# FFN weights gathered in reorder-index order, tokens permuted by one-hot matmuls; norms and scalings of the attention stage on ScalarE

## The chip, the cores and the metric

The kernel runs on one core of one Trainium2 chip, as one launch. A core has five engines with an instruction queue each: TensorE (PE: matmuls and transposes), VectorE (DVE), ScalarE (ACT: activation functions and copies), GpSimd (POOL: elementwise work, and the gathers by index, which it issues), and SyncE (SP), which here only issues DMAs. Each queue runs in the order in which the program was built; queues wait for each other through semaphores. The metric is the device time of one execution in microseconds (us). A run's figure is a median of several executions.

## The reference, cut to what matters

A decoder layer over 4 x 256 = 1024 tokens of width 256: a Mamba block with a mixture of experts, cross attention to 64 context tokens, and an FFN with emulated 8-bit weights and activations. Each is followed by a residual sum and a layernorm. The change touches the last two.

```python
x = layernorm(x + mamba_moe(x))                  # 512 inner channels, 8 experts, top 2
# cross attention, 16 heads of 128
q = rmsnorm((x @ Wq) per head) * gq              # eps 1e-5 inside the rsqrt
k = rmsnorm((ctx @ Wk) per head) * gk
attn = softmax(q @ k.T / sqrt(128))
x = layernorm(x + (attn @ (ctx @ Wv)) @ Wo)
# FFN
def reorder_quantize(x, idx):
    scale = max(abs(x)) / (448 * 6)
    xr = (x / scale)[:, idx]                     # columns gathered by idx
    scale_x = max(abs(xr), per row) / 448
    return fp8(xr / scale_x), scale_x, scale
def qlinear(qx, sx, s, W, idx, out_idx=None):
    Wr = W[:, idx]
    ws = max(abs(Wr), per row) / 448
    y = qx * sx @ (fp8(Wr / ws) * ws).T * s
    return y if out_idx is None else y[:, out_idx]
qx = reorder_quantize(x, up_idx)                 # up_idx: 256 entries
g = qlinear(*qx, w_gate, up_idx, out_idx=down_idx)    # 704 outputs
u = qlinear(*qx, w_up,   up_idx, out_idx=down_idx)
qt = reorder_quantize(silu(g) * u, down_idx)     # down_idx: 704 entries
x = layernorm(x + qlinear(*qt, w_down, down_idx))
```

## The kernel before, in words

Tokens lie in 8 tiles of 128 (`NT`), each token a partition, in `x_sb`. The program is one function, `decoder_kernel`, and runs in stages. A **manual order** (`tc.manual_schedule`) keeps the instructions of PE, DVE, ACT and POOL as they are written in the scan, MoE and combine stages; in the last stage (attention and FFN) the framework's scheduler orders each engine's queue when the program is built.

**Scan** (to about 315 us): the Mamba recurrence, DVE scans with POOL products and PE sums.

**Preparation of K** (`prep_k`, to about 400 us): weights of queries and keys are multiplied together into `m_d` in DRAM, so that scores are one matmul with the tokens. Its last copies `mst` leave by DMA at L785.

**MoE** (about 400 to 613 us): 23 slots (`NSLOT`) of 128 gathered rows. The loop over `s` at L1165 calls `slot_rows` (transposes of the gathered rows, L1109, and two copies, one on ACT, L1111, one on DVE, L1112), `slot_up` (the matmuls `p_gu` at L1121), `slot_act` and `slot_down` (L1144 to L1160). After each slot, `next(fill, None)` runs one piece of `prep_ffn`, which makes the FFN's weights beside the MoE. Its first piece runs ahead of slot 0 (L1163). `prep_ffn` begins with `counts`: an iota on POOL (L949), one-hot matrices of the two index lists on DVE (L962), their column sums on PE (`p_cnt`, L969), which give how often each column is named (`cnt_up`, `cnt_dn`) and a 0/1 mask of those that are named (`mask_up`, `mask_dn`); the transposes `p_cntc` (L977) turn the counts into columns. Then, six times for the up weights (`gather`, `round_gu`, `turn_gu`) and twice for the down weights (`round_dn`, `turn_dn`), the rows are gathered, masked, scaled, rounded, transposed, multiplied by the counts, and written to DRAM as two bf16 parts: a high part and the rest that the product with a count leaves (index j = 0, 1 of `wgu_d`, `wdn_d`). So no token is ever permuted: a column named twice has its weight doubled.

**Combine** (about 613 to 649 us): 16 gathers of expert outputs on POOL's queue (L1214), their sum and a layernorm on DVE, and beside them the matmuls of V and Wo (`prep_v`). SP loads the FFN weights (L1219 to L1222).

**Attention and FFN** (about 649 us to the end): a loop of 11 steps (L1397). Step i runs `stage_scores(i)`, `stage_attend(i - 1)`, `stage_up(i - 2)` and `stage_down(i - 3)`: four tiles are in flight. In one step:

- `stage_scores`: transpose `p_x1T`, ACT copy `x1T` (L1275), query matmuls `p_q` (L1280), squares on ACT (L1285) and sums on DVE (`ssq`, L1286), `rq` = 1/rms (L1290, through `rsqrt_mean`: DVE, DVE, ACT square root), score matmuls `p_sc` (L1295), then the softmax on `v` (128x1024): DVE product (L1302), DVE maximum (L1305), POOL subtraction (L1306), ACT exponential (L1307), DVE sum (L1308), POOL product (L1310).
- `stage_attend`: transposes `p_aT`, ACT copies, matmuls `p_av` (L1327), DVE residual sum (L1330), `layernorm` (L68): statistics, `rsqrt_mean`, and a DVE scaling (L76).
- `stage_up`: POOL mask `xm` (L1347), `quantize` (L1333: maximum, scaling at L1340, `round_fp8` at L78: two DVE operations and two POOL ones), transpose `p_xqT`, ACT copy `xqT` (L1353), matmuls `p_gu` (L1361, 16 of 352 columns), DVE scaling `gu`, SiLU on ACT (L1368), DVE product `tb`.
- `stage_down`: `quantize` of `tb`, transposes `p_tT`, ACT copies `tT`, matmuls `p_fo` (L1386, 12), residual sum, `layernorm`, store.

ACT changes its function table (`ACT_TABLE_LOAD`) whenever it goes between square root, exponential and SiLU; copies need no change.

Of the kernel before, what the change touches and what calls it, by code (L numbers as in the profile page):

```python
# [10 lines left out]
F32 = mybir.dt.float32  # L11
I32 = mybir.dt.int32
AF = mybir.ActivationFunctionType
ALU = mybir.AluOpType
# [3 lines left out]
P = 128  # L18
B, L, D = 4, 256, 256
T = B * L  # L20
NT = T // P
# [28 lines left out]
def decoder_kernel(  # L50
# [17 lines left out]
    def layernorm(buf, t, pool):  # L68

        st = pool.tile([P, 6], F32, tag="ln_st", name="ln_st", bufs=2)  # L70
        mv = pool.tile([P, 2], F32, tag="ln_mv", name="ln_mv", bufs=2)
        rs = pool.tile([P, 1], F32, tag="ln_rs", name="ln_rs", bufs=2)
        nc.vector.bn_stats(st, buf[:, t, :])
        nc.vector.bn_aggr(mv, st)
        rsqrt_mean(rs, mv[:, 1:2], 1, EPS_LN)
        nc.vector.tensor_scalar(buf[:, t, :], buf[:, t, :], mv[:, 0:1], rs, sub, mult)  # L76

    def round_fp8(o, q, m):  # L78
# [6 lines left out]
        nc.gpsimd.tensor_tensor(q, q, m, add)  # L85
        nc.gpsimd.tensor_tensor(o, q, m, sub)
# [47 lines left out]


    mask_up = const.tile([P, D], F32, name="mask_up")
    cnt_up = const.tile([P, KD], F32, name="cnt_up")
    cnt_dn = const.tile([P, NI], F32, name="cnt_dn")
# [566 lines left out]

    wgu_d = dram.tile([2, P, KD, 2, I], BF16, name="wgu_d")
    wdn_d = dram.tile([2, P, NI, D], BF16, name="wdn_d")
# [238 lines left out]
    def counts(ps, pool, mask_dn):  # L946
# [5 lines left out]
        for idx, n, cnt, mask in ((idx_up, D, cnt_up, mask_up), (idx_dn, I, cnt_dn, mask_dn)):  # L952
# [3 lines left out]
            row = pool.tile([P, I], F32, tag="wd_m", name="cntrow")  # L956
            parts = [(0, n)] if n <= HALF else [(0, n // 2), (n // 2, n - n // 2)]
            for o2, w2 in parts:
# [13 lines left out]
                nc.scalar.copy(row[:, o2 : o2 + w2], pt[:, 0:w2])  # L972
            nc.vector.tensor_scalar(mask, row[:, 0:n], 1.0, None, ALU.min)
            yield
            pc = ps.tile([P, HALF], F32, tag="ps", name="p_cntc")
            for i, (o, w) in enumerate(chunks):
                nc.tensor.transpose(pc[:w, i * 32 : i * 32 + 32], row[0:32, o : o + w], ident[0:32, 0:32])  # L977
            for i, (o, w) in enumerate(chunks):
                nc.scalar.copy(cnt[:w, i : i + 1], pc[:w, i * 32 : i * 32 + 1])

    def prep_ffn(fw, ps):

        mask_dn = fw.tile([P, I], F32, name="mask_dn")
        yield from counts(ps, fw, mask_dn)
        mcol = fw.tile([P, NI], F32, name="mcol")
        nc.vector.tensor_scalar(mcol[:, 0 : NI - 1], cnt_dn[:, 0 : NI - 1], 1.0, None, ALU.min)
        nc.vector.tensor_scalar(
            mcol[0 : ICH[-1][1], NI - 1 :], cnt_dn[0 : ICH[-1][1], NI - 1 :], 1.0, None, ALU.min  # L990
        )

        def gather(i):
# [4 lines left out]
                in_offset=bass.IndirectOffsetOnAxis(ap=idx_dn[:w, i : i + 1], axis=0),  # L998
# [3 lines left out]
        def round_gu(i, wt):  # L1002
# [9 lines left out]
            round_fp8(wb[:w], wt[:w], m[:w])  # L1012
            nc.vector.tensor_scalar_mul(sc[:w, 0, 1:2], sc[:w, 0, 1:2], mcol[:w, i : i + 1])
# [4 lines left out]
        def turn_gu(i, wb):  # L1018
# [6 lines left out]
            st = fw.tile([P, 2, KD, 2, P], BF16, tag="w_st", name="w_st", bufs=2)  # L1025
            for k in range(KD):

                src = pt[:, k * 2 * w : (k + 1) * 2 * w].rearrange("p (g o) -> p g o", o=w)
                c = cnt_up[:, k : k + 1]
                nc.vector.tensor_scalar_mul(st[:, 0, k, :, 0:w], src, c)  # L1030
                nc.vector.scalar_tensor_tensor(st[:, 1, k, :, 0:w], src, c, st[:, 0, k, :, 0:w], mult, sub)
            for j in range(2):
                for k in range(KD):
                    nc.sync.dma_start(wgu_d[j, :, k, :, o : o + w], st[:, j, k, :, 0:w])

        def round_dn(r, wt):
# [7 lines left out]
            round_fp8(wb, wt, m)  # L1044
# [3 lines left out]
        def turn_dn(r, wb):  # L1048
# [3 lines left out]
            st = fw.tile([P, 2, NI, P], BF16, tag="wd_st", name="wd_st", bufs=1)  # L1052
            nc.gpsimd.memset(st[I - (NI - 1) * P :, :, NI - 1, :], 0.0)
            for i, (o, w) in enumerate(ICH):
                c = cnt_dn[:w, i : i + 1]
                src = pt[:w, i * P : (i + 1) * P]
                nc.vector.tensor_scalar_mul(st[:w, 0, i, :], src, c)
                nc.vector.scalar_tensor_tensor(st[:w, 1, i, :], src, c, st[:w, 0, i, :], mult, sub)
            for j in range(2):
                nc.sync.dma_start(wdn_d[j, :, :, r * P : (r + 1) * P], st[:, j])  # L1060
# [139 lines left out]
    wgu = [lt2.tile([P, KD, 2, I], BF16, name=f"wgu{j}") for j in range(2)]  # L1200
    wdn = [lt2.tile([P, NI, D], BF16, name=f"wdn{j}") for j in range(2)]
# [5 lines left out]
    with ExitStack() as cctx, tc.manual_schedule(engines={ET.PE, ET.DVE, ET.Activation, ET.Pool}):  # L1207
# [10 lines left out]
        for j in range(2):  # L1218
            nc.sync.dma_start(wgu[j], wgu_d[j])  # L1219
            nc.sync.dma_start(wdn[j], wdn_d[j])  # L1220
        nc.sync.dma_start(sgu_row, sgu_d.unsqueeze(0).to_broadcast([P, 2, I]))
        nc.sync.dma_start(sdn_row, sdn_d.unsqueeze(0).to_broadcast([P, D]))  # L1222
# [35 lines left out]
    with ExitStack() as xctx:  # L1258
# [9 lines left out]
        def stage_scores(t):  # L1268
# [8 lines left out]
            for q in range(H // GQ):  # L1277
# [10 lines left out]
                )  # L1288
            rq = wk2.tile([P, H], F32, tag="rq", name="rq")
            rsqrt_mean(rq, ssq, HD, EPS_A)  # L1290
# [187 lines left out]
```

## Time and profile before

| what | us |
|---|---|
| median of 3 runs (lowest, highest) | 852.98 (850.94, 855.36) |
| the profiled execution, its own time | 856.38 |
| its span, first to last instruction | 854.7 |
| MoE's first expert matmul | 402.12 |
| first query matmul of the last stage | 650.09 |
| query matmuls of tiles 1 to 7 begin | 663.12, 679.59, 698.52, 724.15, 746.23, 768.40, 790.57 |
| busy PE, DVE, ACT, POOL over the span | 685.7, 569.1, 341.4, 385.9 |

The profile is one execution. A page gives busy times and the costliest groups; the chain of work follows the execution back from its last instruction, step by step to what released each; the timeline lists instructions with start and duration in us, and in brackets how long the engine was idle before and what released it. A name such as `xT<-p_xT` is output and inputs, a line number such as L1112 is a line of the kernel before. Ends of matmuls are modelled, and a float32 matmul is listed as two.

### The profile page before, as it was taken

Reading aid. Unit: us, or ns where it says so; the run is one execution under the profiler, and the core shown is the slowest. Engines: PE = TensorE matmul, PEld = TensorE weight load, DVE = VectorE, ACT = ScalarE, POOL = GpSimd, SP = SyncE. Lnnn points to the kernel's source line nnn. Section 1 sums busy time; section 2 is a strip of 40 time slices with the busy share of each in tenths; the row PEclk is TensorE's granted clock in tenths of the full one; section 3 lists DMA queues with packets and bytes.
Section 4 is the critical chain, followed back from the end, with each engine's and each line's share of the span. In section 5 each row is a group of like instructions: output and inputs, shape, how many; then the busy total and the mean of one; then the engine's idle time right before and its main releaser. Section 6 shows DMA issues by size and latency. Waiting matters only on the chain.

```text
span 854.7 us, 8109 instructions
## 1 busy us (share of the span) xinstructions
PE 685.7 (80%) x2449; PEld 383.5 (45%) x2449; DVE 569.1 (67%) x959; ACT 341.4 (40%) x564; POOL 385.9 (45%) x278
## 2 busy tenths in 40 slices
PE   3968868778656776747999999999986998999963
PEld 1533433324322323635555656556642554555541
DVE  4468799997899993663335454555144578888885
ACT  3386654755533323322221112112233555555533
POOL 7039878899766860022012332222060334444451
PEclk9999998999877997767999999999997999999985
DMA  4023322256521308943022544232690101000000
GB/s 153 1 74 86 99 65 69 83 156 205 168 87 44 104 25 298 397 142 104 25 72 17 67 55 66 39 54 56 204 393 16 49 1 49 7 6 7 8 6 19
DMA packets 54954, 76.43 MB, mean 89 GB/s; under 512 B 15872, under 2 KB 35072, under 8 KB 54144
## 3 DMA queue, kind: packets, MB, share of 16 engines
q1 hardware_dynamic: 48048, 64.11, 23.8%
q0 software_dynamic: 2320, 6.56, 5.2%
q10 hardware_dynamic: 4544, 5.24, 1.8%
q8 instruction: 21, 0.34, 0.2%
q14 instruction: 21, 0.17, 0.1%
HBM read 64.22 MB, written 11.67 MB: 89 GB/s over the span
## 4 chain that ended last, share of the span: by engine, by line
PE 45%; DVE 26%; POOL 12%; issue 7%; ACT 6%; DMA 3%; ACTq 0%; POOLq 0%; DVEq 0%
PE p_gu L1121 12%; PE p_hTb L1151 8%; DVE hs L654 6%; PE py L644 5%; POOL dbx L595 4%; PE p_q L1280 3%; PE p_m L774 2%; DVE hc L662 2%; PE p_cv L264 2%; POOL v L1306 1%; PE p_gu L1361 1%; DMA wk_t<-in_wk_dram 1%; POOL yg L1214 1%; PE p_sc L1295 1%; DVE ssq L1286 1%
## 5 line engine op out<-in xcount | busy, mean ns | idle before, releaser
L595 POOL TENSOR_TENSOR dbx<-dtx,bB 128x1024 f32<-128x1024 f32 x64 | 149.4, 2354 | 23.7 <-DVE hs L654 12.5
L654 DVE TENSOR_TENSOR_SCAN hs<-da,dbx 128x1024 f32<-128x1024 f32 x64 | 145.5, 2281 | 17.0 <-POOL dbx L595 8.6
L644 PE MATMUL py<-hc,ident 128*128 128x512 f32 x256 | 134.1, 656 | 3.6 <-DVE yd L615 2.0
L1121 PE MATMUL p_gu<-w,xT 128*128 x276 | 119.2, 569 | 2.0 <-ACT xT L1111 2.0
L587 ACT ACTIVATE da<-dt,a_neg 128x510 f32<-128x510 f32 x128 | 87.7, 688 | 77.6 <-DVE hs L654 75.4
L644 PEld LDWEIGHTS py<-hc,ident 128*128 128x128 f32 x256 | 52.9, 208 | 113.8 <-issue 101.0
L606 PE MATMUL pC<-bc,sel 96*128 96x512 bf16 x50 | 20.5, 409 | 66.1 <-DVE hc L662 65.3
L1121 PEld LDWEIGHTS p_gu<-w,xT 128*128 128x128 f32 x276 | 49.9, 194 | 44.0 <-issue 34.6
L1151 PE MATMUL p_hTb<-w2r,hT 128*128 (+1 forms) x276 | 67.9, 387 | 0.7 <-ACT hT L1140 0.7
L662 DVE TENSOR_TENSOR hc<-hs,pC 128x1024 f32<-128x1024 f32 x50 | 61.1, 1221 | 4.8
L1280 PE MATMUL p_q<-wq_sb,x1T 128*128 128x512 f32 x128 | 58.8, 613 | 4.8 <-ACT x1T L1275 4.8
L1151 PEld LDWEIGHTS p_hTb<-w2r,hT 128*128 128x128 f32 (+1 forms) x276 | 50.4, 189 | 19.1 <-issue 7.6
L1132 DVE TENSOR_TENSOR h<-sg,p_gu 128x704 f32<-128x704 f32 x23 | 20.4, 888 | 42.1 <-ACT sg L1130 42.1
L1140 ACT COPY hT<-p_hTa 128x512 f32<-128x512 f32 x23 | 13.5, 586 | 83.1 <-PE p_hTa L1139 76.0
L917 POOL DMA_INDIRECT xs<-flat_d,tok_i x23 | 22.7, 986 | 43.0 <-PE p_xT L1109 28.4
L1280 PEld LDWEIGHTS p_q<-wq_sb,x1T 128*128 128x128 f32 x128 | 24.4, 195 | 34.6 <-issue 26.9
L85 POOL TENSOR_TENSOR wgu<-wgu,w_m 128x512 f32<-128x512 f32 (+1 forms) x6 | 7.6, 1267 | 71.3 <-DVE w_m L84 71.3
L1147 DVE COPY hT<-p_hTb 128x128 f32<-128x128 f32 (+1 forms) x46 | 11.0, 281 | 41.4 <-PE p_hTb L1144 41.4
L679 POOL TENSOR_TENSOR hc<-hs,cB 128x1024 f32<-128x1024 f32 x14 | 32.9, 2350 | 8.9 <-issue 5.3
L1306 POOL TENSOR_TENSOR v<-v,st 128x1024 f32<-128x1024 f32 x8 | 15.2, 1902 | 48.0 <-DVE st L1305 48.0
L1285 ACT ACTIVATE q<-p_q 128x512 f32<-128x512 f32 x32 | 18.9, 594 | 34.1 <-PE p_q L1280 26.5
L1214 POOL DMA_INDIRECT yg<-ys_d,yrow_i x16 | 15.4, 965 | 37.2 <-PE p_vT L814 32.6
(331 smaller groups left out, 1278.0 us busy)
## 6 DMA issues: line engine op xcount, KB each, us to landing
bB<-b_d SPq DMA_DIRECT2D x64, 256.0 KB, 3.2
w<-in_w1T_dram SPq DMA_DIRECT2D x2, 2816.0 KB, 21.5
w<-in_w3T_dram SPq DMA_DIRECT2D x2, 2816.0 KB, 25.3
w2r<-in_w2T_dram SPq DMA_DIRECT2D x8, 640.0 KB, 5.6
m_d<-mst SPq DMA_DIRECT2D x8, 512.0 KB, 2.9
mb<-m_d SPq DMA_DIRECT2D x4, 1024.0 KB, 8.2
cB<-b_d SPq DMA_DIRECT2D x14, 256.0 KB, 3.3
ys_d<-y SPq DMA_DIRECT2D x21, 128.0 KB, 1.7
```

The lines of the kernel that those rows point to most:

```text
L587: nc.scalar.activation(das[i % 2][:, j, :, 1:], dt[:, c, cs].rearrange("p (b l) -> p b l", l=L)[:, :, 1:], AF.Exp, scale=a_neg[:, c * N + ...
L595: nc.gpsimd.tensor_tensor(dbxs[i], dtx[:, c0 : c0 + 2, h * HALF : (h + 1) * HALF], bBs.pop(i).unsqueeze(1).to_broadcast(two), mult)
L644: nc.tensor.matmul(ys[i][j], ident, hc[:, j, :], start=(n == 0), stop=(n == N - 1))
L654: nc.vector.tensor_tensor_scan(hs, das[i % 2].rearrange("p c b l -> p (c b l)"), dbxs.pop(i).rearrange("p c t -> p (c t)"), 0.0, mult, add,)
L662: nc.vector.tensor_tensor(hcs[i], hv, pcs.pop(i).unsqueeze(1).to_broadcast(two), mult)
L679: nc.gpsimd.tensor_tensor(hcs[i], hv, cBs.pop(i).unsqueeze(1).to_broadcast(two), mult)
L917: nc.gpsimd.indirect_dma_start(out=xs[s], out_offset=None, in_=flat_d, in_offset=bass.IndirectOffsetOnAxis(ap=tok_i[:, s : s + 1], axis=0),)
L1121: nc.tensor.matmul(pt[:, c, 0:w], x[:, k, :], w13[k][:, bass.DynSlice(ex[s], 1), o : o + w].rearrange("p e i -> p (e i)"), start=(k == 0), ...
L1151: nc.tensor.matmul(po, hT[:w, i, :], w2r[:w, i, bass.DynSlice(ex[s], 1), :].rearrange("p e d -> p (e d)"), start=(i == 0), stop=(i == NI - 1),
L1214: nc.gpsimd.indirect_dma_start(out=y, out_offset=None, in_=ys_d, in_offset=bass.IndirectOffsetOnAxis(ap=yrow_i[:, j, t : t + 1], axis=0),)
L1280: nc.tensor.matmul(pq, x1T[:, k, :], wq_sb[:, k, q * HALF : (q + 1) * HALF], start=(k == 0), stop=(k == KD - 1),)
L1306: nc.gpsimd.tensor_tensor(v, v, st[:, 0].unsqueeze(2).to_broadcast(full), sub)
```

## The change

Line numbers here are those of the kernel before, unless said otherwise.

1. `counts` becomes `masks`: no counts, no `p_cntc` transposes; the one-hot matrices of `up_idx` are transposed (`p_pm`) and stored to DRAM as `pm_d`.
2. `prep_ffn` composes the down index with itself: three DVE operations and six gathers of one 4-byte element per partition, on POOL's queue, ahead of the iota; the up weights' rows are gathered by that index `dd`.
3. The weights are no longer multiplied by counts and have no low part: one ACT copy in place of the DVE operations, and half as many stores.
4. `load_ffn` in place of the four loads at L1219 and L1220: two gathers of `wgu` by `up_idx` and six of `wdn` by `down_idx` on POOL's queue, behind the 16 gathers of the combine stage; SP loads `pm` and the two scale rows.
5. `stage_up` permutes the quantized tokens with four matmuls `p_xp` (128 columns each) and one more ACT copy `xpT`; `p_gu` has 8 matmuls a tile instead of 16, `p_fo` 6 instead of 12.
6. `layernorm` takes the root on ACT first, then DVE's reciprocal, and scales on ACT; `rq` likewise; `quantize` scales on ACT. For the last tile, softmax and rounding run on DVE instead of POOL.

```diff
@@ layernorm, round_fp8
-        rsqrt_mean(rs, mv[:, 1:2], 1, EPS_LN)
-        nc.vector.tensor_scalar(buf[:, t, :], buf[:, t, :], mv[:, 0:1], rs, sub, mult)
+        nc.scalar.activation(rs[:, 0:1], mv[:, 1:2], AF.Sqrt, bias=eps_ln)
+        nc.vector.reciprocal(rs[:, 0:1], rs[:, 0:1])
+        nc.vector.scalar_tensor_tensor(rs[:, 1:2], mv[:, 0:1], -1.0, rs[:, 0:1], mult, mult)
+        nc.scalar.activation(buf[:, t, :], buf[:, t, :], AF.Identity, scale=rs[:, 0:1], bias=rs[:, 1:2])
...
-        nc.gpsimd.tensor_tensor(q, q, m, add)
-        nc.gpsimd.tensor_tensor(o, q, m, sub)
+        eng.tensor_tensor(q, q, m, add)
+        eng.tensor_tensor(o, q, m, sub)
@@ counts -> masks
-                nc.scalar.copy(row[:, o2 : o2 + w2], pt[:, 0:w2])
-            nc.vector.tensor_scalar(mask, row[:, 0:n], 1.0, None, ALU.min)
-            yield
-            pc = ps.tile([P, HALF], F32, tag="ps", name="p_cntc")
-            for i, (o, w) in enumerate(chunks):
-                nc.tensor.transpose(pc[:w, i * 32 : i * 32 + 32], row[0:32, o : o + w], ident[0:32, 0:32])
-            for i, (o, w) in enumerate(chunks):
-                nc.scalar.copy(cnt[:w, i : i + 1], pc[:w, i * 32 : i * 32 + 1])
+                if n == D:
+                    pm = ps.tile([P, 2 * HALF], BF16, tag="ps", name="p_pm")
+                    for k in range(KD):
+                        for i in range(KD):
+                            nc.tensor.transpose(
+                                pm[:, k * D + i * P : k * D + (i + 1) * P], ohs[i][:, k * P : (k + 1) * P], identb
+                            )
+                    pmt = pool.tile([P, KD, D], BF16, tag="w_st", name="pmt", bufs=2)
+                    nc.scalar.copy(pmt.rearrange("p k i -> p (k i)"), pm[:, 0 : KD * D])
+                    nc.sync.dma_start(pm_d, pmt)
+                nc.vector.tensor_scalar(mask[:, o2 : o2 + w2], pt[:, 0:w2], 1.0, None, ALU.min)
@@ prep_ffn
+        at = fw.tile([P, 2, NI], I32, name="at")
+        nc.vector.tensor_single_scalar(at[:, 0], idx_dn, 7, op=ALU.arith_shift_right)
+        nc.vector.tensor_single_scalar(at[:, 1], idx_dn, P - 1, op=ALU.bitwise_and)
+        dd_at = fw.tile([P, NI], I32, name="dd_at")
+        nc.vector.scalar_tensor_tensor(dd_at, at[:, 1], float(NI), at[:, 0], mult, add)
+        dd = fw.tile([P, NI], I32, name="dd")
+        for i in range(NI):
+            nc.gpsimd.indirect_dma_start(
+                out=dd[:, i : i + 1], out_offset=None, in_=dn_idx.rearrange("p (i one) -> (p i) one", one=1),
+                in_offset=bass.IndirectOffsetOnAxis(ap=dd_at[:, i : i + 1], axis=0),
+            )
         mask_dn = fw.tile([P, I], F32, name="mask_dn")
-        yield from counts(ps, fw, mask_dn)
...
+        yield from masks(ps, fw, mask_dn)
@@ turn_gu (turn_dn alike)
+            nc.scalar.copy(
+                st[:, :, :, 0:w], pt[:, 0 : 2 * KD * w].rearrange("p (k g o) -> p k g o", g=2, o=w)
+            )
             for k in range(KD):
...
-                nc.vector.tensor_scalar_mul(st[:, 0, k, :, 0:w], src, c)
-                nc.vector.scalar_tensor_tensor(st[:, 1, k, :, 0:w], src, c, st[:, 0, k, :, 0:w], mult, sub)
...
@@ load_ffn, called behind the gathers of the combine stage
+        nc.sync.dma_start(pm, pm_d)
+        nc.sync.dma_start(sgu_row, sgu_d.unsqueeze(0).to_broadcast([P, 2, I]))
+        nc.sync.dma_start(sdn_row, sdn_d.unsqueeze(0).to_broadcast([P, D]))
+        for k in range(KD):
+            nc.gpsimd.indirect_dma_start(
+                out=wgu[:, k].rearrange("p g o -> p (g o)"), out_offset=None, in_=wgu_d,
+                in_offset=bass.IndirectOffsetOnAxis(ap=idx_up[:, k : k + 1], axis=0),
+            )
+        for i, (o, w) in enumerate(ICH):
+            nc.gpsimd.indirect_dma_start(
+                out=wdn[:w, i, :], out_offset=None, in_=wdn_d,
+                in_offset=bass.IndirectOffsetOnAxis(ap=idx_dn[:w, i : i + 1], axis=0),
+            )
@@ stage_scores
-            rsqrt_mean(rq, ssq, HD, EPS_A)
-            nc.vector.tensor_scalar_mul(rq, rq, 1.0 / math.sqrt(HD))
+            nc.scalar.activation(rq, ssq, AF.Sqrt, bias=eps_q)
+            nc.vector.reciprocal(rq, rq)
...
-            nc.gpsimd.tensor_tensor(v, v, st[:, 0].unsqueeze(2).to_broadcast(full), sub)
+            eng = nc.gpsimd if t < NT - 1 else nc.vector
+            eng.tensor_tensor(v, v, st[:, 0].unsqueeze(2).to_broadcast(full), sub)
...
@@ quantize
-            nc.vector.tensor_scalar_mul(f, src, sc[:, 1:2])
-            round_fp8(q, f, m)
+            nc.scalar.activation(f, src, AF.Copy, scale=sc[:, 1:2])
+            round_fp8(q, f, m, eng)
@@ stage_up
+            pp = ps.tile([P, HALF], F32, tag="ps", name="p_xp")
+            for i in range(KD):
+                for k in range(KD):
+                    nc.tensor.matmul(
+                        pp[:, i * P : (i + 1) * P], pm[:, k, i * P : (i + 1) * P], xqT[:, k, :],
+                        start=(k == 0), stop=(k == KD - 1),
+                    )
+            xpT = wk2.tile([P, KD, P], BF16, tag="xpT", name="xpT")
+            nc.scalar.copy(xpT.rearrange("p k t -> p (k t)"), pp[:, 0 : KD * P])
...
-                        for j in range(2):
-                            nc.tensor.matmul(
-                                pg[:, g, 0:HI], xqT[:, k, :], wgu[j][:, k, g, hs],
-                                start=(k == 0 and j == 0), stop=(k == KD - 1 and j == 1),
-                            )
+                        nc.tensor.matmul(
+                            pg[:, g, 0:HI], xpT[:, k, :], wgu[:, k, g, hs], start=(k == 0), stop=(k == KD - 1)
+                        )
...
```

## The prediction

> **What bounds the kernel now.** I read the page's chain of waits first, then its order in time, then the timeline of one step of the last stage and of the start of the MoE, because the change puts work at just these two places. In the last stage the chain, in order of time, reads:
>
> ```profile
> 754.97 1.50 DVE rq L64
> 759.94 1.91 POOL v L1306
> 763.24 1.38 PE p_gu L1361 x8
> 777.14 1.51 DVE rq L64
> 782.11 1.91 POOL v L1306
> 785.42 1.38 PE p_gu L1361 x8
> ```
>
> The same three names return every 22.17 us. PE is busy for some 27 of each 30 us there, so it looks like the bound, but the chain is a ring through four engines: scores, DVE, POOL's subtraction, the exponential, then `xqT`, `p_gu`, SiLU, `x1T` and the next tile's queries. ACT's part of the ring stands in its timeline:
>
> ```profile
> 761.87 1.06 ACT L1307 ACTIVATE v<-v 128x1024 f32<-128x1024 f32 x1 [2.23 <-POOL v L1306]
> 762.83 0.35 ACT L1353 COPY xqT<-p_xqT 128x256 bf16<-128x256 bf16 x1
> 763.09 0.70 ACT L1381 COPY tT<-p_tT 128x640 bf16<-128x640 bf16 x1
> 763.67 0.26 ACT L1382 COPY tT<-p_tT 64x128 bf16<-64x128 bf16 x1
> 763.95 1.28 ACT L66 ACT_TABLE_LOAD   x1
> 765.24 0.20 ACT L66 ACTIVATE ln_rs<-ln_rs 128x1 f32<-128x1 f32 x1
> 765.46 1.28 ACT L1368 ACT_TABLE_LOAD   x1
> 766.76 1.33 ACT L1368 ACTIVATE f_s<-gu,sx 128x352 f32<-128x352 f32 x2
> 767.99 0.35 ACT L1275 COPY x1T<-p_x1T 128x256 f32<-128x256 f32 x1
> ```
>
> From the exponential's start to its end there is nothing between it and `xqT`; from then to `x1T` ACT hardly rests. The next `p_q` starts at 768.40, behind the last line. PE waits 0.9 us for `xqT` and 0.9 us for `x1T` in a step: it is nearly, not quite, the bound, and ACT's order decides. At the start of the MoE:
>
> ```profile
> 402.07 0.72 POOL L949 IOTA iota<- 128x704 f32 x1 [15.74 <-DVE idf L955]
> 402.82 0.62 DVE L962 TENSOR_SCALAR onehot<-iota,idf 128x256 bf16<-128x256 f32 x2 [0.93 <-POOL iota L949]
> 402.94 1.08 POOL L917 DMA_INDIRECT xs<-flat_d,tok_i  x1 [0.15 <-issue]
> 403.35 0.60 DVE L1112 TENSOR_SCALAR xT<-p_xT,pk 128x128 f32<-128x128 f32 x2
> 403.75 0.58 PEld L1121 LDWEIGHTS p_gu<-w,xT 128*128 128x128 f32 x2 [1.13 <-DVE xT L1112]
> ```
>
> POOL's iota holds DVE's one-hots, these hold DVE's `xT`, and that holds PE. A gather costs POOL the same for rows of 1 KB and 2 KB:
>
> ```profile
> 472.82 0.95 POOL L996 DMA_INDIRECT wgu<-in_w_gu_dram,idx_dn  x1 [0.30 <-issue]
> 623.49 0.95 POOL L1214 DMA_INDIRECT yg<-ys_d,yrow_i  x1 [0.30 <-issue]
> ```
>
> **What the Trainium skill says.** "ScalarE: Activation LUTs", What ACT_TABLE_LOAD costs, has 1283 ns for a load, and a drain of 1380 ns with it. The trace agrees on the load (1.28) and shows no drain: the activation follows 0.01 us later. "SBUF — State Buffer", Who interferes with whom: DVE's two-port operations and POOL exclude each other for whole instructions. The trace agrees: `rq` at L64, 128x16 elements, starts at 754.97 and lasts 1.50, until POOL's `tq` ends at 756.44. "DMA: Bandwidth & Descriptors", SWDGE vs HWDGE vs iDMA: descriptors of POOL's DMAs are computed by software on its cores; the 0.95 above, equal for both sizes, fits. "TensorE: Matmul & The Clock Gate", What's actually happening: PE falls to half clock after an idle window of some 3.4 us; here `p_q` of tile 0, after 7.5 us idle, took 8.92 against 7.13.
>
> **The change, part by part.** The order of each queue in the changed program is known from the build; durations are from the trace.
>
> *Start of the MoE.* POOL's queue now has six `dd` gathers ahead of the iota, and they wait for three small DVE operations (0.15 to 0.2 each), which like `idf` now can't start before 401.72. Queued behind the gathers: the iota, so the one-hots, so `xT` on DVE, so all of PE. Six gathers of 0.95 + 0.30 are 7.5, the DVE operations about 0.5, of which 0.2 is hidden: **+7.8**. No row shows a gather of 4 bytes. From below, only 0.30 each (+2.1 in all), from above 1.39 each, the spacing at 402.94 (+8.7); a gain is excluded, since nothing is taken from this path. I take 1.25, as size made no difference.
>
> *Rest of the MoE.* The two slots with `p_cntc` last 9.16 and 9.12 against 8.53 of a slot without filling: -1.2 when they go. Four `p_pm` transposes beside `p_cnt` add about 0.1. `turn_gu` keeps its transposes, and its four DVE operations (0.34 and 0.49, twice) become one ACT copy (0.6); PE-bound slots hide both, as DVE is busy for 45% there and ACT for 23%: 0 (0.4 a slot, eight slots, if the cover went). Half the stores go from SP; nobody waits for them: 0. Sum **-1.1**.
>
> *Combine.* Eight gathers more on POOL, 10 us, behind the 16: POOL ends near 652 instead of 642. Its next work is `v` at 665, and `p_gu` first wants the weights at 696: 0, hidden by 13 us of POOL's idleness. SP loses four loads (2.2 MB) and gains `pm`: 0.
>
> *One full step of the last stage.* Time counts from the start of `p_q`. Before: `v` at 11.08, exponential ends 16.70, `p_q` again at 22.17. After:
> - `ssq` is ready at 8.7 as before. ACT root 0.22, DVE reciprocal 0.25; no two-port operation meets `tq`. So `v` waits for `p_sc` alone (10.4): 10.6. This gains 0.5.
> - `v` 1.23, maximum 1.22, POOL 1.90 with its hops: exponential 15.1 to 16.2.
> - ACT's next instructions are now the table load and the root of the layernorm: 1.28 + 0.20, to 17.7. Only then `xqT` (0.35), 18.0; then the layernorm's scaling, which waits for DVE's softmax sum (1.22 from 16.2), two reciprocals and a product, to 18.3, and lasts 0.40 (the row of 128x256 squares on ACT has 0.40): 18.7; then `xpT`, 19.05. `p_xp` is between: four matmuls of 128 columns, between 0.06 (issue distance of `p_xqT`) and 0.14 each (its listed mean of two); I take 0.08.
> - POOL: the softmax product 1.90 from 18.0, then `xm` 0.73: 20.75. DVE: maximum 0.42, two scalars: 21.5. ACT waits for this with `x_f` (0.40), *ahead of* SiLU: 22.0. Table load 1.28: 23.3. Two SiLU, 1.1, and `x1T`: `p_q` at **24.6**.
> - `p_gu` (8 x 0.16) and `p_fo` (6 x 0.13) save 2.06 of PE's time, `p_xp` takes 0.32; all of it falls into the wait for ACT. DVE loses the scalings (1.0 + 0.6 + 0.3 a step and more while POOL holds the port); no path wants them.
>
> So a step costs +2.4. The same walk for the other steps: tile 1 to 2 has only `x1T` behind load and root, +1.4; 2 to 3 adds scaling and `xpT`, +1.6; 3 to 4 takes 25.63 now, and 24.6 then, -1.0; three full steps +7.2. Sum **+9.2**.
>
> *Tail*, from the last tile's `p_q` to the end (64.1): subtraction on DVE 1.2 for POOL's 1.9 and a hop, -0.8; rounding of the last `xq` -0.75 and `tq` -1.6 (3.39 on POOL against two of 0.9); half of the cold `p_gu` (4.88) that leads to the first `gu`, -1.2; half of the cold last `p_fo` (2.85), -1.4; `p_xp`, `xpT` and hops, 0.9 for each of three tiles, +2.7. Sum **-3.1**.
>
> *Clock.* PE now rests from 15.6 to 19.1 but for 0.9 us, and from 21.5 to 24.6. Half clock for one window costs `p_q` 1.7; from below 0. In five steps I take **+1.1** in all, up to +8.
>
> Total 7.8 - 1.1 + 9.2 - 3.1 + 1.1 = +13.9. Against the profiled execution's own 856.4 this is 870.3; that execution lies 3.4 above the median of the runs, 852.98, so the median should be **867**.
>
> **The rivals.** (a) *PE is the bound of the last stage after all.* For it: PE is busy for nine tenths, and waits only 1.8 of 22.17. Then 8 x (2.06 - 0.32) = 13.9 go, and 2.4 of the tail's rounding; with +6.7 from the MoE 843: faster. It decides from the point where ACT reaches `x1T` before PE's `p_fo` is over, 1.7 earlier than now; against it stands the built order, which puts a table load, a root, a scaling and `x_f` into this very stretch of ACT. (b) *The short gathers are cheap or overlap*, 0.30 each: 867 - 5.7 = 861. Against: 0.95 at both sizes. (c) *The last stage comes out even*, because a table load is partly hidden as some are now, and the tail gains more: 853 + 6.7 = 860. For it: DVE is freed of 2 to 3 us a step, and small reorderings of a ring are easily misjudged. (A change that isn't in effect is excluded: its instructions stand in the built queues.)
>
> **How the numbers follow.** Forecast 0.66 (860 to 876), (a) 0.08, (b) 0.13, (c) 0.13. A difference of 0.5%, 4.3 us, is about what a measurement of this kernel can tell from no change. Above 857.3 lie all of the forecast but a little, and most of (b) and (c): slower 0.82, same 0.10, faster 0.08. The range 857 to 876 leaves out (a), the lower tails of (b) and (c), and a clock worse than +8.
>
> **What would show it.** Right: PE's first expert matmuls some 7.8 us later, with six gathers on POOL before the iota; steps of 24 to 25 us between `p_q`; PE waiting for `x1T` about 3 us a step, and on ACT a table load between exponential and `xqT`. Wrong: steps under 22.2, or gathers of `dd` at well under 0.9; a step above 25.5 with cold `p_q` means that the clock was underrated.

## The result and the profile after

The changed kernel takes 881.38 us (median of 4 runs, 879.69 to 885.28) against 853.48 for the kernel before: **ratio 1.0313, interval 1.0283 to 1.0344**. It is slower, as forecast, but by 27.9 us where 13.9 were forecast, and outside the range given. Ratios, here and below, leave out executions that took over 1.5% longer than the fastest of their kernel; medians do not (in the variants below, seven of e10's twenty executions and two of e6's twenty are of this kind).

The spans of the two profiled executions are 854.7 and 878.0, 23.3 apart. (The remaining 4.6 lie in which execution was profiled: 2.9 above its median before, 1.7 below it after.) Where they lie, read from the start of PE's groups in the two timelines:

| stretch | before | after | difference | forecast |
|---|---|---|---|---|
| start to the MoE's first expert matmul | 402.12 | 399.24 | -2.9 | 0 |
| from there to `p_cnt`, behind the first slot's rows | 7.71 | 16.51 | +8.8 | +7.8 |
| `p_cnt` to tile 0's `p_q` (rest of the MoE, combine) | 240.26 | 239.79 | -0.5 | -1.1 |
| tile 0's `p_q` to tile 7's (seven steps) | 140.48 | 157.73 | +17.2 | +9.2, and most of 1.1 for the clock |
| tile 7's `p_q` to the end | 64.13 | 64.73 | +0.6 | -3.1 |

The chain of waits after, in order of time (start, us, what), one full step and the beginning of the next:

```profile
788.47 7.13 PE p_q L1301 x16
795.60 3.45 PE p_sc L1317 x8
...
801.70 1.91 POOL v L1329
...
806.57 1.89 POOL v L1333
...
809.98 1.58 DVE gu L1397 x2
...
813.27 8.83 PE p_q L1301 x16
```

After POOL's first operation (the subtraction) the chain now goes through its second one (the softmax product) and through `gu`; before, it went from the exponential and `xqT` straight to `p_gu`. `x_f` and SiLU wait for these. And the two `p_q` are not of one length: 7.13 and 8.83. ACT's timeline of that step (idle before, and releaser, in brackets):

```profile
803.63 1.06 ACT L1330 ACTIVATE v<-v 128x1024 f32<-128x1024 f32 x1 [1.75 <-POOL v L1329]
804.71 1.28 ACT L75 ACT_TABLE_LOAD   x1
806.00 0.29 ACT L75 ACTIVATE ln_rs<-ln_mv,eps_ln 128x1 f32<-128x1 f32 x1
806.21 0.35 ACT L1376 COPY xqT<-p_xqT 128x256 bf16<-128x256 bf16 x1
806.72 0.60 ACT L78 ACTIVATE x_sb<-x_sb,ln_rs 128x256 f32<-128x256 f32 x1 [0.17 <-DVE ln_rs L77]
807.23 0.35 ACT L1386 CAST xpT<-p_xp 128x256 bf16<-128x256 f32 x1
...
810.07 0.51 ACT L1363 ACTIVATE x_f<-xm,sx 128x256 f32<-128x256 f32 x1 [1.58 <-DVE sx L93]
810.60 1.28 ACT L1399 ACT_TABLE_LOAD   x1
811.89 1.07 ACT L1399 ACTIVATE f_s<-gu,sx 128x352 f32<-128x352 f32 x2
812.87 0.35 ACT L1296 COPY x1T<-p_x1T 128x256 f32<-128x256 f32 x1
```

This is the order that the prediction walked through: `xqT` behind a load and a root, `x_f` ahead of SiLU, `x1T` last. PE's side of it, from the middle to the next queries:

```profile
803.71 0.28 PE L1374 MATMUL p_xqT<-identb,xq 128*128 128x128 bf16 x2
806.61 0.38 PE L1381 MATMUL p_xp<-xqT,pm 128*128 128x128 bf16 x4 [2.63 <-ACT xqT L1376]
806.83 0.78 PE L1409 MATMUL p_tT<-identb,tq 128*128 128x128 bf16 x6
807.64 2.53 PE L1393 MATMUL p_gu<-wgu,xpT 128*128 128x352 bf16 x8
...
813.27 8.83 PE L1301 MATMUL p_q<-wq_sb,x1T 128*128 128x512 f32 x16 [1.77 <-ACT x1T L1296]
```

And in the kernel before:

```profile
746.23 7.13 PE L1280 MATMUL p_q<-wq_sb,x1T 128*128 128x512 f32 x16 [0.88 <-ACT x1T L1275]
...
763.24 2.56 PE L1361 MATMUL p_gu<-wgu,xqT 128*128 128x352 bf16 x16 [1.05 <-ACT xqT L1353]
```

PE rested for 1.05 and 0.88 in a step before; now it rests for 2.63, then 1.77 ahead of `p_q`, and the 8 matmuls of `p_gu` take 2.53, about as long as 16 of them did. The clock column of stretches of 3.4 us, two earlier steps (columns: stretch, its length, then busy time with instructions of PE, PE's weight loads, DVE, ACT and POOL, granted PE clock, DMA share, GB/s), shows why:

```profile
752.40:755.80 3.40, 0.78 (x12) 0.64 (x10) 2.64 (x7) 3.20 (x5) 0.56 (x1) 1.00 0.00 0
755.80:759.20 3.40, 3.28 (x15) 1.74 (x13) 1.26 (x4) 1.72 (x5) 2.04 (x2) 0.51 0.02 5
759.20:762.60 3.40, 1.68 (x9) 0.82 (x8) 3.40 (x9) 3.35 (x6) 0.98 (x2) 0.99 0.00 0
762.60:766.00 3.40, 3.40 (x6) 1.36 (x5) 2.65 (x9) 1.72 (x4) 0.63 (x1) 0.51 0.00 0
...
786.57:789.98 3.41, 1.84 (x6) 0.88 (x7) 3.41 (x8) 3.12 (x5) 1.61 (x2) 1.00 0.00 0
789.98:793.39 3.41, 3.41 (x10) 1.50 (x9) 2.46 (x9) 2.58 (x5) 0.00 (x0) 1.00 0.07 22
```

A stretch in which PE is busy for 0.78 or 1.68 of 3.4 is followed by one at half clock; one with 1.84 is not, and the query matmuls that start in it, those of tile 6, are warm ("warm" is at full clock, 7.1 us; "cold" wholly or partly at half clock). Each full step has two rests; it depends on how they fall into the stretches whether one or two of these follow at half clock. At the start of the MoE, POOL and then DVE and PE:

```profile
406.46 0.95 POOL L997 DMA_INDIRECT dd<-in_dn_idx_dram,dd_at  x1 [0.30 <-issue]
407.41 0.75 POOL L951 IOTA iota<- 128x704 f32 x1
408.19 0.61 DVE L963 TENSOR_SCALAR onehot<-iota,idf 128x256 bf16<-128x256 f32 x2 [8.83 <-POOL iota L951]
...
408.73 0.60 DVE L1119 TENSOR_SCALAR xT<-p_xT,pk 128x128 f32<-128x128 f32 x2
...
409.12 6.79 PE L1128 MATMUL p_gu<-w,xT 128*128 x10 [7.81 <-DVE xT L1119]
```

This is the last of the six gathers, each 1.25 behind the other, and the wait of 7.81 that they make. Before, these first twelve matmuls ran in one piece (402.12, 7.87 long).

### The profile page after: what moved, and what is told of

It reads as the page before. It is cut to its first block, busy times and chain, and to the rows that moved or that the text cites. A ratio compares the mean times of both kernels' runs of the same rounds, so it can differ in the third digit from the quotient of the medians.

```text
span 878.0 us, 7858 instructions
## 1 busy us (share of the span) xinstructions
PE 681.6 (78%) x2365; PEld 376.8 (43%) x2365; DVE 534.8 (61%) x867; ACT 368.8 (42%) x604; POOL 389.0 (44%) x284
## 4 chain that ended last, share of the span: by engine, by line
PE 50%; DVE 20%; POOL 12%; ACT 8%; issue 6%; DMA 3%; POOLq 0%; ACTq 0%; DVEq 0%
PE p_gu L1128 11%; PE p_q L1301 8%; PE p_hTb L1158 7%; DVE hs L656 6%; POOL dbx L597 4%; PE py L646 4%; PE p_sc L1317 3%; POOL yg L1239 2%; PE p_m L776 2%; PE p_cv L266 2%; DVE hc L664 1%; PE p_av L1350 1%; DMA wk_t<-in_wk_dram 1%; POOL v L1329 1%; PE p_hTa L1146 1%
## 5 line engine op out<-in xcount | busy, mean ns | idle before, releaser
L597 POOL TENSOR_TENSOR dbx<-dtx,bB 128x1024 f32<-128x1024 f32 x64 | 149.5, 2359 | 23.6 <-DVE hs L656 12.3
L1301 PE MATMUL p_q<-wq_sb,x1T 128*128 128x512 f32 x128 | 66.5, 680 | 10.6 <-ACT x1T L1296 10.6
L664 DVE TENSOR_TENSOR hc<-hs,pC 128x1024 f32<-128x1024 f32 x50 | 61.1, 1221 | 5.2 <-DVE hs L656 0.5
L1301 PEld LDWEIGHTS p_q<-wq_sb,x1T 128*128 128x128 f32 x128 | 27.5, 220 | 45.3 <-issue 31.7
L1307 DVE TENSOR_REDUCE ssq<-q 128x4 f32<-128x512 f32 x32 | 21.8, 682 | 22.3 <-ACT q L1306 22.3
L1137 ACT ACTIVATE sg<-p_gu 128x704 f32<-128x704 f32 x23 | 17.4, 757 | 36.9 <-PE p_gu L1128 36.9
```

Source lines behind the costliest of these rows:

```text
L597: nc.gpsimd.tensor_tensor(dbxs[i], dtx[:, c0 : c0 + 2, h * HALF : (h + 1) * HALF], bBs.pop(i).unsqueeze(1).to_broadcast(two), mult)
L664: nc.vector.tensor_tensor(hcs[i], hv, pcs.pop(i).unsqueeze(1).to_broadcast(two), mult)
L1301: nc.tensor.matmul(pq, x1T[:, k, :], wq_sb[:, k, q * HALF : (q + 1) * HALF], start=(k == 0), stop=(k == KD - 1),)
```

## The experiments

The theory after the result: (1) six gathers hold the MoE's start; (2) ACT's order makes the warm step 24.8; (3) PE's two rests a step bring half clock, which costs what the forecast lacked. Rivals: one part alone makes the loss; the hop through `p_xp` lengthens the ring; the slow clock has other causes. All ratios are to the kernel before, run beside them; it had medians of 855.4 to 856.7 there, so a median of e1 to e12 is not to be set against 853.48. The steps and tails are from one profile each.

| run | median | ratio (interval) | steps, tile 0 to 7 | last three | tail |
|---|---|---|---|---|---|
| before | 853.48 | | 140.5 | 22.08, 22.17, 22.17 | 64.1 |
| changed | 881.38 | 1.0313 (1.0283-1.0344) | 157.7 | 26.35, 26.50, 24.80 | 64.7 |
| e1_dd_early | 873.39 | 1.0182 (1.0108-1.0257) | 157.2 | 26.27, 26.50, 24.79 | 64.8 |
| e2_norms_only | 870.06 | 1.0149 (1.0106-1.0193) | 149.9 | 24.56, 22.95, 24.63 | 65.6 |
| e3_ffn_only | 870.46 | 1.0141 (1.0081-1.0200) | 151.4 | 24.67, 24.16, 24.19 | 64.6 |
| e4_warm | 885.61 | 1.0319 (1.0270-1.0367) | 156.5 | 26.29, 26.49, 24.81 | 65.5 |
| e5_warm2 | 883.48 | 1.0343 (1.0276-1.0410) | 153.6 | 24.71, 26.50, 24.80 | 66.7 |
| e6_ln_dve_early | 860.74 | 1.0063 (1.0037-1.0089) | 145.8 | 25.47, 24.16, 24.16 | 67.3 |
| e7_x1_ahead | 850.71 | 0.9945 (0.9906-0.9985) | 135.7 | 21.26, 22.49, 21.77 | 63.8 |
| e8_norms_x1_ahead | 847.07 | 0.9908 (0.9878-0.9937) | 129.3 | 20.44, 20.73, 20.44 | 65.6 |
| e9_quant_dve | 866.54 | 1.0134 (1.0104-1.0165) | 151.7 | 24.02, 24.02, 24.02 | 61.1 |
| e10_before_x1_ahead | 857.13 | 0.9981 (0.9954-1.0008) | 137.7 | 20.98, 22.09, 23.76 | 65.9 |
| e11_warm3 | 875.02 | 1.0235 (1.0192-1.0278) | 154.3 | 24.70, 24.80, 24.80 | 63.2 |
| e12_x1_quant_dve | 849.42 | 0.9916 (0.9880-0.9951) | 135.9 | 22.27, 21.26, 21.26 | 60.9 |

**e1_dd_early: the gathers at another place.**

```diff
@@ behind run(kv), the end of the preparation of K; their indices are computed at the kernel's start
+        for i in range(NI):
+            nc.gpsimd.indirect_dma_start(
+                out=dd[:, i : i + 1], out_offset=None, in_=dn_idx.rearrange("p (i one) -> (p i) one", one=1),
+                in_offset=bass.IndirectOffsetOnAxis(ap=dd_at[:, i : i + 1], axis=0),
+            )
```

> The changed kernel, but the six short gathers that compose the down index stand on GpSimd's queue behind the last copies of the preparation of K, before the wait that opens the MoE, and their three VectorE operations at the kernel's start. If the gathers cost the path what they take on GpSimd (1.25 us each), PE's first long run of expert matmuls starts about 7.5 to 8.5 us earlier against the first expert matmul than in the changed kernel, the steps of the last stage stay as they are, and the time falls from 881.4 to about 873. If the gathers were overlapped or if another wait stands right behind them, the time stays above 878.

The ratio falls from 1.0313 to 1.0182. POOL's timeline:

```profile
393.03 0.95 POOL L953 DMA_INDIRECT dd<-in_dn_idx_dram,dd_at  x1 [0.30 <-issue]
402.41 0.72 POOL L962 IOTA iota<- 128x704 f32 x1 [8.43 <-DVE idf L968]
```

The last gather is out 8.43 before POOL may start the iota. From the first expert matmul to `p_cnt` it is 7.73 (7.71 before, 16.51 changed). The gathers cost 8.8, all of it by their place: 7.8 of wait and 1.0 because more of the matmuls behind it ran at half clock. This second part varies: the same stretch took 15.2 to 16.9 in the profiles with the gathers at the old place and 7.2 to 8.7 in those without.

**e2_norms_only and e3_ffn_only: one part each.** e2 is the kernel before with part 6 alone; e3 is the changed kernel with part 6 undone:

```diff
@@ e3: layernorm, rq, quantize as before
-        nc.scalar.activation(buf[:, t, :], buf[:, t, :], AF.Identity, scale=rs[:, 0:1], bias=rs[:, 1:2])
+        nc.vector.tensor_scalar(buf[:, t, :], buf[:, t, :], mv[:, 0:1], rs[:, 0:1], sub, mult)
...
-            nc.scalar.activation(f, src, AF.Copy, scale=sc[:, 1:2])
+            nc.vector.tensor_scalar_mul(f, src, sc[:, 1:2])
```

> The kernel before with part 6 of the change alone (norms, rq and the scalings on ScalarE, the last tile's softmax and rounding on VectorE); the FFN weights keep counts and low parts. The theory that the loss of the last stage comes from ScalarE's order (a table load, a root and scalings in the ring) and from PE's cold windows says: here x_f stands behind x1T in the built order, and p_gu is twice as long, so steps of about 22.5 to 23.5 with warm query matmuls (7.1), a tail shorter by 2 to 3: 850 to 858. The rival that moving norms and scalings to ScalarE costs the ring by itself, whatever the FFN does, says steps of 24 to 25 and 862 or more.

> The changed kernel with part 6 undone (norms, rq and scalings on VectorE, rounding of the last tile on GpSimd); the FFN's gathered weights, the permutation matmuls and the gathers of dd stay. Theory: +8 from the gathers at the MoE's start, steps of 22.2 to 22.5 if PE stays warm, but PE has 14 us less to do and waits in each step, so some query matmuls are cold (8.8 for 7.1): 861 to 870. The rival that ScalarE's order alone makes the loss of the last stage, with the clock no part of it, says warm query matmuls and about 860.

For e2 the theory as I had put it fell: 870, not 850 to 858. Its queries from tile 3 on are warm and one of its full steps is 22.95, as expected, but a table load and a root stand between exponential and `xqT` here as well, PE rests 2.18 there, and the half clock that follows now falls on `p_gu` in every other step (PE's timeline, two steps):

```profile
748.75 4.18 PE L1368 MATMUL p_gu<-wgu,xqT 128*128 128x352 bf16 x16 [2.18 <-ACT xqT L1360]
...
773.32 2.56 PE L1368 MATMUL p_gu<-wgu,xqT 128*128 128x352 bf16 x16 [2.18 <-ACT xqT L1360]
```

The same 16 matmuls take 1.6 longer, and the step is 24.6 instead of 22.95. Besides, the step from tile 2 to 3 took 23.8 (18.9 before), with the query of tile 2 cold (8.75), and the tail became 1.5 longer, not 2 to 3 shorter. So the rival written down for this run, that norms and scalings on ScalarE cost the ring by themselves, came true in its numbers. e3 came out 0.5 above the range expected, with the query matmuls of its last four tiles cold (8.68 to 9.34); a step of 24.2 less 1.7 is 22.5. One step of it, 3 to 4, took 29.95, for a reason that is its own: ACT's queue there has the SiLU, and so its wait for DVE's `gu`, ahead of `tT`. So neither part alone is to blame: +9.5 and +11.0 in the steps, +17.2 together.

**e4_warm, e5_warm2, e11_warm3: PE kept busy.** Transposes that nobody reads are added to the changed kernel: nothing is taken away, PE gets more work.

```diff
@@ stage_up, behind the transposes p_xqT (e4: 20; e5: 38; e11: 38, but none for the last two tiles)
+            for n in range(38):
+                c = (2 + n % 6) * P
+                nc.tensor.transpose(pt[:, c : c + P], xq[:, 0:P], identb)
@@ stage_scores (e4: 6, in the tile of p_x1T; e5: 11, in that of p_q; e11: 24 for tiles 4 to 7, 20 for tile 2)
+                for n in range(11 if q == 0 else 0):
+                    c = (n % 4) * P
+                    nc.tensor.transpose(pq[:, c : c + P], x_sb[:, t, 0:P], ident)
```

> The changed kernel with 26 more transposes per tile on PE, whose results nobody reads: 20 in bf16 behind p_xqT, where PE waits 2.6 us for xqT, and 6 in float32 behind p_x1T, where it waits 1.6 to 2.1 us for x1T. If the cold query matmuls (8.7 to 9.5 for 7.1) come from these two rests, they become warm, the steps of 26.4 become 24.8, and the time falls by 5 to 8, to about 875. If the clock is not at fault (or PE itself is the bound), the time stays or rises by up to 3 us, to 881 to 885.

> The first try with extra transposes (e4_warm) filled PE's rests only in part: its 26 transposes took 2.1 us, and rests of 1.5 and 0.9 to 2.5 us a step remained; the half-clock stretches of the last stage's full steps fell from nine to four. Here the changed kernel gets 38 in bf16 behind p_xqT and 11 in float32 ahead of the query matmuls, in their own tile, so that they need not wait for ScalarE's copy x1T and it not for them. If the cold query matmuls come from PE's rests, all those of tiles 2 to 7 are warm (7.1) and the steps of the last stage sum to about 151 to 153 (157.7 in the changed kernel). If they do not, steps of 26.4 remain, and the sum stays at 156 or more.

> e5_warm2 with the rest ahead of the query matmuls filled altogether: 24 float32 transposes for tiles 4 to 7 and 20 for tile 2 (11 left 1.94 us of rest, more than half of a window of 3.4), none for the other tiles, and none behind p_xqT for the last two tiles, whose tail e5_warm2 had made 5 longer. If the half clock comes from rests over half a window, every query matmul of tiles 2 to 7 takes 7.1, the four full steps are 24.7 to 25 each, the time from tile 0's to tile 7's query matmuls is 150 to 152, the tail 63 to 64, and the time 872 to 876. If not, cold ones remain, and it is 880 or more.

e4 missed: I had overrated the length of a transpose (20 took 1.28, 6 took 0.82), and rests of up to 2.5 were left. e5 cured the queries of tiles 2, 3 and 4 (7.0 to 7.1), not those of 5 and 7 (8.83). In its profile, which is of its fastest execution, the steps are 4.2 shorter in sum and the tail is 2.0 longer; its median and ratio are not below those of the changed kernel. Where cold queries stayed, 1.94 of a window of 3.4 was still rest. e11 fills that too. Its PE before a query, and the clock of the stretches around it:

```profile
757.73 2.78 PE L1302 MATMUL p_q<-ident,x_sb 128*128 128x128 f32 x24
761.03 7.13 PE L1304 MATMUL p_q<-wq_sb,x1T 128*128 128x512 f32 x16 [0.52 <-ACT x1T L1296]
```

```profile
757.30:760.70 3.40, 3.22 (x28) 2.86 (x27) 3.33 (x10) 2.83 (x5) 0.10 (x1) 1.00 0.00 0
760.70:764.10 3.40, 3.06 (x7) 1.44 (x8) 3.30 (x9) 1.95 (x5) 1.51 (x2) 1.00 0.00 0
```

All queries of tiles 2 to 7 now take 7.0 to 7.1, and the full steps are 24.7 to 24.8 instead of up to 26.5. With *more* PE work, steps and tail together are 5.0 shorter (217.5 against 222.5), and the ratio falls from 1.0313 to 1.0235. The sum of steps, 154.3, stayed above the 150 to 152 expected because of step 3 to 4, 27.8 against 25.2. There a one-column VectorE operation of the layernorm (`ln_rs`, L77) took 1.76 instead of 0.16 beside POOL's `v`; PE waited 1.80 for `xpT`, `p_gu` behind it ran at half clock (2.53), and the added transposes ended only at 736.3, though `x1T` was ready at 734.4. So the clock is a cause, and PE's work is not the bound.

**e6_ln_dve_early and e9_quant_dve: which of ACT's instructions.** Both are e1 with one piece of part 6 undone: the layernorm, or the scaling of `quantize`; the lines are those of the diff under e3.

> e1_dd_early with the layernorm again as in the kernel before (root through rsqrt_mean, scaling on VectorE); quantize and rq stay on ScalarE. In the built order ScalarE's table load for the layernorm then stands behind xqT and xpT, no scaling waits ahead of xpT, and x_f stands behind x1T. If that order makes the ring, the warm step is 22.2 to 22.5 where it is 24.8 in e1_dd_early, the steps sum to 139 to 147 depending on how many windows are cold, and the time falls from about 873 to 855 to 864. The rival that the hop through p_xp and xpT makes the ring longer says steps of 24 or more and 868 or more.

> e1_dd_early with the scaling of quantize (x_f, t_f) again on VectorE, layernorm and rq still on ScalarE: in the built order ScalarE goes from tT straight to the table load for SiLU, without x_f ahead of it. The prediction had x_f hold the table load from 21.5 to 22.0 of a step. If x_f is what holds x1T, the warm step falls from 24.8 to 23 or less. If the layernorm's load, root and scaling are what counts, as e6_ln_dve_early says, the warm step is 24.2 to 24.6, query matmuls are still cold, and the time is 868 to 874.

e6: 860.7, with its last four queries cold. No full step of it is warm; its 24.16 less 1.70, what a cold query adds elsewhere, is 22.46: the layernorm's load, root and scaling, with `x_f`, which the scheduler now puts behind `x1T`, are worth 2.3 of the 24.8. The hop through `p_xp` and `xpT` is still there, so the rival that it makes a warm step of 24 or more falls. Why it is no better shows in PE's timeline:

```profile
759.39 0.38 PE L1379 MATMUL p_xp<-xqT,pm 128*128 128x128 bf16 x4 [1.02 <-ACT xqT L1374]
...
765.06 0.28 PE L1414 MATMUL p_fo<-wdn,tT 64*128 64x256 bf16 x1 [2.68 <-ACT tT L1411]
```

PE's queue is stopped by the last `p_fo`, whose 64-row piece of `tT` now stands behind SiLU; and its tail is 2.5 longer than that of e1, which I did not follow up. e9 came out somewhat below its expectation: steps of 24.02 where 24.2 to 24.6 were expected, and warm queries from tile 4 on where cold ones were expected. Its half clock falls on `p_gu` (2.2 to 2.3), behind which PE waits for ACT anyway. So `x_f` is worth 0.8, the smaller part of the ring. Its larger effect is in the tail, 61.1 against 64.8: 1.7 of that is the warm query of the last tile, 2.0 are left for ACT's scalings. (e12 against e7, both with a warm last query, gives 2.9 for them.) One place of the tail, ACT after the last `p_xqT`, of the changed kernel and of e9:

```profile
852.99 1.28 ACT L75 ACT_TABLE_LOAD   x1 [3.28 <-DVE st_t L92]
854.28 0.29 ACT L75 ACTIVATE ln_rs<-ln_mv,eps_ln 128x1 f32<-128x1 f32 x1
854.48 0.35 ACT L1376 COPY xqT<-p_xqT 128x256 bf16<-128x256 bf16 x1
854.74 0.88 ACT L1363 ACTIVATE t_f<-tb,st_t 128x704 f32<-128x704 f32 x1
```

```profile
836.80 0.37 ACT L1376 COPY xqT<-p_xqT 128x256 bf16<-128x256 bf16 x1 [3.48 <-PE p_xqT L1374]
837.19 1.28 ACT L75 ACT_TABLE_LOAD   x1
```

In the first, the load goes ahead of `xqT`, and `t_f` waits behind it; in e9 `xqT` goes out when its transposes are done.

**e7, e8, e10, e12: `x1T` a step earlier.** The next tile's `x1T` needs only the combine's `x_sb`, so it may be made behind this tile's scores:

```diff
-                vs[i] = stage_scores(i)
+                if i == 0:
+                    turn_x1(0)        # p_x1T and the copy x1T, taken out of stage_scores
+                vs[i] = stage_scores(i)
+                if i + 1 < NT:
+                    turn_x1(i + 1)
```

e7 has it on e1, e8 on e2, e10 on the kernel before, e12 on e1 with `quantize` on VectorE.

> e1_dd_early with one change of order: the transposes p_x1T of the next tile and their copy x1T are issued right behind the scores of the tile before, since they need only the combine's result. PE's next query matmuls then wait for PE alone, not for ScalarE's x_f, table load, SiLU and x1T. If ScalarE's queue ahead of x1T ends the step, steps become 20.5 to 22.5 and the time 848 to 862. If another thing bounds the step (PE, VectorE or the softmax), steps stay at 24 or more and the time at 868 or more.

> e2_norms_only (FFN weights as before, norms and scalings on ScalarE) with the same early x1T. PE keeps all its work, so it stays warm; its busy time of a step is 20.4. If the wait for x1T is what norms and scalings on ScalarE made longer, steps are 20.4 to 21.5, and the time is 2% below the kernel before (0.975 to 0.99). If they cost elsewhere, steps stay at 23 to 24.5 and the time is above the kernel before.

> The kernel before with nothing but the early x1T of e7 and e8. Worked out from the order of the built queues with the durations of the profile: the next query matmuls no longer wait for ScalarE's SiLU and x1T, but rq is still made by five small operations, four of them on VectorE behind wide ones, so the softmax starts later and the steps are 22 to 23: the same as the kernel before (0.99 to 1.005). If the wait for x1T is the whole of it, whatever rq and norms do, steps are 20.4 to 21 and the ratio is that of e8_norms_x1_ahead, 0.99 or less.

> e7_x1_ahead (early gathers of dd, early x1T, all FFN changes, layernorm and rq on ScalarE) with the scaling of quantize on VectorE, as in e9_quant_dve. e9 took 3.7 from the tail of e1 and 0.8 from each full step. Here the steps should be 20.4 to 21.5 instead of 21.3 to 22.5, and the tail 60 to 62 instead of 63.8, so the time about 4 to 6 below e7's 850.7: 844 to 847, ratio 0.985 to 0.992. If x1T's early copy has already taken away what quantize cost, only the tail gains, and the ratio stays within 0.992 to 0.995.

e7 is 22.7 below e1, e8 23.0 below e2, and both come out a little below the kernel before: by 0.5%, about what the prediction gave as the least that can be told from no change, and by 0.9%. e8's ratio, 0.9908, misses the expected 0.975 to 0.99 by little; its steps are in the range. ACT's timeline of e7 shows two things at once:

```profile
775.71 0.37 ACT L1296 COPY x1T<-p_x1T 128x256 f32<-128x256 f32 x1 [0.55 <-PE p_x1T L1295]
...
780.73 1.06 ACT L1336 ACTIVATE v<-v 128x1024 f32<-128x1024 f32 x1 [2.20 <-POOL v L1335]
781.69 0.35 ACT L1382 COPY xqT<-p_xqT 128x256 bf16<-128x256 bf16 x1
782.06 1.28 ACT L75 ACT_TABLE_LOAD   x1
```

`x1T` is out of the way before the exponential, and the scheduler now also puts the load behind `xqT`. The 3.3 between 24.8 and some 21.5 belong to both; I did not part them. e10 has the early `x1T` without part 6 and gains nothing measurable: 0.9981, with full steps of 21.0 to 23.8. DVE's timeline shows the likely reason:

```profile
750.72 1.03 DVE L64 TENSOR_SCALAR rq<-ssq 128x16 f32<-128x16 f32 x1
751.79 0.25 DVE L65 RECIPROCAL rq<-rq 128x16 f32<-128x16 f32 x1
752.32 1.18 DVE L1297 TENSOR_SCALAR rq<-rq 128x16 f32<-128x16 f32 x1 [0.28 <-ACT rq L66]
753.61 1.22 DVE L1308 TENSOR_TENSOR v<-p_sc,rq 128x1024 f32<-128x1024 f32 x1
```

Two operations on 16 elements take 1.03 and 1.18, beside POOL's two rounding operations for `tq` (750.04 to 753.48), and `v` starts 12.3 behind `p_q` (741.35); in the changed kernel it is 10.6. (`rq` is made by four operations, three of them on VectorE; I had counted one too many.) So part 6 as a whole is of use once `x1T` no longer waits, as e8 against e10 shows; that it is its `rq` is read from this timeline, not tested alone. e12 had the shorter tail (60.9), but its steps sum to what e7's do, and its time, 849.4, misses the 844 to 847 expected; its ratio, 0.9916, can't be told from e7's or e8's.

## Why the prediction was right in direction and wrong in size

- *Start of the MoE*, +7.8: right, the wait of PE was 7.81 and 1.25 a gather held for 4 bytes too. Not counted: 1.0 of half clock after it.
- *Rest of the MoE*, -1.1, and *combine*, 0: -0.5 together, in the changed kernel and in e1.
- *One full step*: 24.6 forecast, **24.8** measured warm (e11, and the warm step of the changed kernel). 1 to 2: +1.4 forecast, +1.6. 3 to 4: -1.0, and 25.25 less 0.55 of a cold query is -0.9. 2 to 3: +1.6, and +1.4 in e11, where PE stays warm there; in the changed kernel it is +4.2, of which 1.7 are the cold query and 1.2 `p_gu` at half clock (2.53 for 1.37), directly ahead of `p_q` on PE's queue. The walk by queue order and durations held: with the cold queries (6.0) and this `p_gu` taken out, the changed kernel's seven steps are +10.0 against +9.2.
- ***Clock***, "In five steps I take +1.1 in all, up to +8": **this is the term that failed**. It was mis-sized, not missing. Cold queries cost 0.5 + 1.7 + 0.55 + 1.6 + 1.7 in the steps and 1.7 in the tail, `p_gu` of step 2 to 3 1.2, and the cold matmuls of the MoE's start 1.0: 9.9 in all, nine times the value taken and above the bound. The prediction had written the two rests down, 3.5 less 0.9 and 3.1, and that half clock follows an idle window of some 3.4; I took a value near the lower bound, with no working for it. The sign it gave for this, a step above 25.5 with cold `p_q`, came twice (26.35 and 26.50). The Trainium skill ("TensorE: Matmul & The Clock Gate", HAM oscillation) speaks of idle gaps above about 3.4 as the ones to avoid. The measured rests were shorter, 2.6 and 1.6 to 2.1 (the second because `p_gu` and `p_fo` ahead of it ran slower), and enough: a window in which PE was busy for 1.68 of 3.4 was followed by half clock. The measurement decides here. The transposes of e11 confirm it from the other side.
- *Tail*, -3.1: +0.6. 1.7 is the cold query; the other 2.0 go with `quantize`'s scalings on ACT (e9, without them and with a warm last query, has a tail 3.1 shorter than that of the kernel before), which the prediction let the last tiles have for nothing.
- The stretch ahead of the MoE, and which executions were profiled, moved the rest: -2.9 and +4.6. Together: clock +8.8 over the forecast, ring +0.8, tail +2.0, rest of the MoE +0.6, these two +1.7, which is the 13.9 or 14.0 that the forecast lacked. Without the clock's 8.8 the result would have lain inside the range.

Rival (a), PE as the bound, is refuted by e11, where more work for PE made it faster; (b) by the 1.25 of each gather; (c) by the result itself, and by e1, whose last stage alone is 17.4 longer than before.

## What to carry to other kernels

When a change takes work from a PE that was nearly full, price its rests: here PE waited twice a step for about half a clock window and paid with slower work, 8.9 us in the last stage, while the 14 us of matmuls that were saved gained nothing. A step that is moved to a queue costs by what stands behind it there: look for the copy that feeds the next round and bring that forward first; with that and the early gathers, the same change that had cost 3% came out 0.5% below the kernel before. A group of short gathers costs its issue time on GpSimd (1.25 us each here), so put it where GpSimd waits anyway.

## What the runs showed that I had not expected

- PE need not be idle for a whole window: half of one was enough. The last stage of all fourteen profiles, from 655 to 840 us, has 659 windows of 3.41 at full clock, cut where the clock itself changes. In the 68 that half clock followed, PE was busy for at most 1.71; in the others it was busy for 1.72 or more, with one exception (1.58, e9).
- Half clock hits what comes next, so such a rest costs `p_q` 1.7 in one build, `p_gu` 1.6 in another (e2), and next to nothing where PE waits for ACT afterwards (e9). The Trainium skill (same page, What's actually happening) has the window free-running, and e9 agrees: the half-clock stretches of its four full steps come 23.9 apart, seven windows of 3.41, beside steps of 24.02.
- The start of the MoE's first expert matmul lay between 396.5 (e6) and 407.0 (e4), though what stands ahead of it is nearly the same in all builds. A difference of a few us between two single executions is no evidence; differences by stage are.
